# Triangle's sides made with tokens on partitions, half of them kept in SBUF

## The chip, the cores and the metric

The kernel runs on one core of a Trainium2 chip. A core has a matrix engine (TensorE, "PE" in the profile, its weight loads "PEld"), a vector engine (VectorE, "DVE"), an activation engine (ScalarE, "ACT"), GpSimd ("POOL"), a synchronising engine that mostly issues transfers (SyncE, "SP"), and 16 DMA engines that all of them share. The on-chip memories are SBUF and PSUM, each of 128 partitions; TensorE writes PSUM only. The metric is device time in microseconds for one execution. It is given as the median of several runs, and the profile is of one execution more.

## The reference

The input x is one image of 512 by 512 places with 64 channels. Two layers are added to it in turn, each on a group-normalised copy (32 groups, so two channels share a mean and a variance over the whole image).

The first layer is a triangle product. For each place, with LN a normalisation over the 64 channels:

```python
xn = LN(GN(x)) * norm_w + norm_b
m = sequence_mask                                   # 512 numbers, 0 or 1
left  = (xn @ left_w  + left_b)  * m[k] * m[j] * sigmoid(xn @ lgate_w + lgate_b)
right = (xn @ right_w + right_b) * m[k] * m[i] * sigmoid(xn @ rgate_w + rgate_b)
out[i, j, d] = sum over k of left[k, j, d] * right[k, i, d]
out = LN(out) @ out_w + out_b
x = x + out * sigmoid(xn @ ogate_w + ogate_b)
```

(with `onorm` scale and shift in the second LN). The second layer takes a two-dimensional Fourier transform of GN(x), keeps 12 by 12 modes, mixes the channels of each mode with complex weights, transforms back and adds the result.

About half of the mask's 512 entries are one. If at most 256 are, only those rows and columns make `left` and `right`, and the kernel takes its compact path: they are numbered as K = 256 slots. Rows and columns that are masked out get the same constant, the row of `out_b`, in place of a product.

## The kernel before

P is 128, C is 64, K is 256, N is 512. The compact path goes through these stages, each with its order of instructions written out by hand for every engine.

**Index stage** (lines 73 to 137). The mask is counted with a matmul; `n_i` is the number of valid rows and decides between the two paths; `rank_p` numbers the rows, valid ones first; `src_i` and `slot_row` are the resulting lists of rows and slots.

**Gathering stage** (lines 656 to 701). Sixteen tiles `jc` of 32 columns are gathered by GpSimd (`xg` for the two first blocks of ranked rows, `yg` for the two others). TensorE turns every piece into PSUM (L687), VectorE takes its statistics (L688), and ScalarE and GpSimd copy the columns that have a slot into `xc`, a tile of 128 partitions by 257 slots by 2 rows by 64 channels (L673). After tile 8, `make_weights` (L171) folds the norm's scale, shift and mean into the weights. At the end `ab1` holds the group norm's scale and shift of each channel.

**Slots' stage** (lines 704 to 810). `xc` is walked in 64 groups `q` of 4 slots (2 rows a partition: 512 tokens in columns). `channels` turns a group so that channels lie on partitions (rows r = 0, 1 in the two halves of 64) and applies the group norm on ScalarE; `centered` multiplies by a centring matrix, squares, and VectorE sums over channels (L800); every four groups `factors` makes reciprocal roots in nine steps on VectorE, and `spread` sends them by way of HBM (`rs_d`) to all channels (`rbc`). `normed` multiplies (L762), `project` makes gates and sides as 64 x 128 weights against 512 tokens (L768), ScalarE takes the sigmoid with the bias of each partition (L778), VectorE adds the bias to the sides and multiplies (L795), and SP stores `left` and `right` to HBM (L807) with a channel as the outer dimension. The first kind of work on a group runs 13 groups ahead of `project`, the lead-in. The tiles `gates_c`, `sides_c` and `sigc` are single.

**The gap.** After the stage come the bias rows, the two matrices `center_x` and `gate_x`, and the mask in the forms `mask_s` and `mask_own` (lines 813 to 853).

**Triangle** (lines 854 to 915). For every channel `c` both sides are loaded back from HBM four to six channels ahead, turned by eight transposes (L873), copied to SBUF (`left_t` by VectorE L879, `right_t` with the mask by ScalarE L883), and multiplied by four matmuls of 128 x 128 by 256 (L895); VectorE evicts with the masks (L900); SP stores to `tri_d` (L903).

**Products' stage** (lines 990 to 1290, the first 8 of `total_g / 8` rounds). `tri_d` is loaded by channel (`load_product`, L1025), multiplied by a centring matrix and `out_w` (`y_ps`, L1058), normalised, and stored as `u_d`. The units that follow are 32 pieces of the image: each is gathered three units ahead (`load`, called at L1241 to L1245), gets its output gate, is multiplied with `u_d` or the constant row, added to x, stored, and given to the Fourier sums. The tail (from L1316) adds the second layer and writes the output.

TensorE's fp32 matmul appears as two passes (records) in the profile, a transpose as one.

## Time and profile before

| | |
|---|---|
| median of 3 runs | 1782.21 us (1778.42 to 1784.91) |
| profiled execution | 1777.78 us, its span 1776.0 us |
| index and gathering stages | to 200.3 us in the span |
| Slots' stage, lead-in | 200.3 to 227.0 |
| Slots' stage, 64 groups | 227.0 to 440.4 |
| gap before the first triangle product | 440.4 to 453.2 |
| triangle | 453.2 to 619.0 |
| products' stage | 624.6 to 730 |
| units and tail | to 1776.0 |
| busy: TensorE, VectorE, ScalarE, GpSimd | 1567.8, 1413.7, 933.0, 936.5 us |

Reading: a busy share is an average over stages with different limits, so each stage is read by itself, with the waits that end last there. Matmuls are pipelined, so the time of one includes what overlaps with the next; the pitch of a group or a channel says more than the duration of one matmul. A line of groups gives count, total busy time, mean of one in ns, and the idle time before it with what ended it.

### The profile page before, as it was taken

Reading aid. Unit: us, or ns where it says so; the run is one execution under the profiler, and the core shown is the slowest. Engines: PE = TensorE matmul, PEld = TensorE weight load, DVE = VectorE, ACT = ScalarE, POOL = GpSimd, SP = SyncE. Lnnn points to the kernel's source line nnn. Section 1 sums busy time; section 2 is a strip of 40 time slices with the busy share of each in tenths; the row PEclk is TensorE's granted clock in tenths of the full one; section 3 lists DMA queues with packets and bytes.
Section 4 is the critical chain, followed back from the end, with each engine's and each line's share of the span. In section 5 each row is a group of like instructions: output and inputs, shape, how many; then the busy total and the mean of one; then the engine's idle time right before and its main releaser. Section 6 shows DMA issues by size and latency. Waiting matters only on the chain. (4 is left out here: it accounts for less than half of the span.)

```text
span 1776.0 us, 32619 instructions
## 1 busy us (share of the span) xinstructions
PE 1567.8 (88%) x10918; PEld 1242.0 (70%) x10918; DVE 1413.7 (80%) x2982; ACT 933.0 (53%) x1660; POOL 936.5 (53%) x695
## 2 busy tenths in 40 slices
PE   6779799997999978899999999999999977998772
PEld 5667666662899867787888888888888745665341
DVE  7989678887455568688999999999999984865451
ACT  3666566663333266676777777777777742011000
POOL 4666211111000037698999999999999881111110
PEclk9999999999899999899999999999999976555555
DMA  7999278878898789868767767776776699999999
GB/s 281 386 386 388 107 206 227 229 229 245 279 305 303 257 246 347 298 196 296 265 242 257 253 233 259 264 249 239 249 264 244 212 318 400 425 427 427 426 427 385
DMA packets 192593, 518.48 MB, mean 292 GB/s; under 512 B 37664, under 2 KB 104480, under 8 KB 151456
## 3 DMA queue, kind: packets, MB, share of 16 engines
q1 hardware_dynamic: 156112, 295.65, 47.5%
q0 software_dynamic: 32832, 218.45, 33.4%
q10 hardware_dynamic: 3472, 2.20, 0.5%
q8 instruction: 89, 1.46, 0.3%
q14 instruction: 88, 0.72, 0.1%
HBM read 311.60 MB, written 204.60 MB: 291 GB/s over the span
## 5 line engine op out<-in xcount | busy, mean ns | idle before, releaser
L1045 PE MATMUL w_ps<-gate_x,xt_c 128*128 128x128 f32 x2048 | 280.5, 281 | 30.0 <-DVE z_t L1274 28.6
L1113 POOL TENSOR_TENSOR places<-places,z_t 128x1024 f32<-128x1024 f32 x127 | 301.3, 2372 | 8.0
L1045 PEld LDWEIGHTS w_ps<-gate_x,xt_c 128*128 128x128 f32 x2048 | 252.0, 194 | 46.4 <-DVE z_t L1274 44.6
L1045 PE MATMUL c_ps<-center_x,xt_c 128*128 128x128 f32 x2048 | 277.0, 279 | 0.8 <-ACT xt_c L1040 0.4
L1045 PEld LDWEIGHTS c_ps<-center_x,xt_c 128*128 128x128 f32 x2048 | 252.8, 194 | 3.8 <-ACT xt_c L1040 3.0
L1440 PE MATMUL l_ps<-places,rinv 24*128 24x512 f32 x512 | 206.2, 1118 | 29.3 <-DVE places L1447 19.0
L1168 DVE BATCH_NORM_STATS2 stats2c<-places 128x6 f32<-128x128 f32 x1024 | 220.5, 278 | 9.9 <-POOL places L1113 9.9
L1083 DVE TENSOR_REDUCE scratch<-sq_c 128x16 f32<-128x1024 f32 x160 | 194.6, 1216 | 31.1 <-ACT sq_c L1078 16.1
L1221 ACT ACTIVATE z_t<-z_t 128x1024 f32<-128x1024 f32 x128 | 135.5, 1058 | 131.8 <-DVE z_t L1280 131.1
L1440 PEld LDWEIGHTS l_ps<-places,rinv 24*128 24x128 f32 x512 | 119.8, 302 | 110.8 <-DVE places L1447 56.9
L1278 POOL TENSOR_TENSOR z_t<-z_t,bias_row_out 128x1024 f32<-128x1024 f32 x32 | 75.6, 2363 | 226.3 <-PE y_ps L1058 202.1
L1040 ACT ACTIVATE xt_c<-t_ps,ab_xc 128x512 f32<-128x512 f32 x256 | 176.0, 688 | 11.5 <-PE t_ps L1038 10.6
L1274 DVE TENSOR_TENSOR z_t<-w_ps,rs_n 128x512 f32<-128x512 f32 x256 | 172.0, 672 | 6.2 <-PE w_ps L1045 6.1
L1076 ACT ACTIVATE sq_c<-c_ps 128x512 f32<-128x512 f32 x256 | 150.8, 589 | 31.4 <-PE c_ps L1045 30.8
L1280 DVE TENSOR_TENSOR z_t<-z_t,scratch 128x1024 f32<-128x1024 f32 x128 | 156.3, 1221 | 9.9 <-ACT rs_n L1089 3.7
L688 DVE BATCH_NORM_STATS2 stats1c<-x_ps 128x6 f32<-128x512 f32 x256 | 157.1, 682 | 7.7 <-PE x_ps L687 7.4
L1109 POOL TENSOR_TENSOR z_t<-z_t,places 128x1024 f32<-128x1024 f32 x64 | 151.8, 2371 | 14.6 <-ACT z_t L1221 14.4
L1038 PE MATMUL t_ps<-c_ident,places 128*128 128x128 f32 x1024 | 158.4, 278 | 0.0
L1038 PEld LDWEIGHTS t_ps<-c_ident,places 128*128 128x128 f32 x1024 | 118.5, 142 | 51.4 <-issue 51.4
L1447 DVE TENSOR_TENSOR places<-places,l_ps 128x512 f32<-128x512 f32 x176 | 109.3, 682 | 55.2 <-DMA places<-x_h,dst_i 42.1
L1109 POOL TENSOR_TENSOR z_t<-z_t,bias_row_out 128x1024 f32<-128x1024 f32 x63 | 149.4, 2372 | 5.8 <-ACT z_t L1221 5.5
L673 ACT COPY xc<-xg 128x128 f32 x352 | 105.0, 298 | 66.1 <-POOL xc L673 47.1
(214 smaller groups left out, 2557.0 us busy)
## 6 DMA issues: line engine op xcount, KB each, us to landing
x_h<-places SPq DMA_DIRECT2D x64, 1024.0 KB
out_x<-places SPq DMA_DIRECT2D x44, 1024.0 KB
places<-u_d SPq DMA_DIRECT2D x512, 64.0 KB
out_x<-lx_t SPq DMA_DIRECT2D x20, 1024.0 KB
rbc<-rs_d POOLq DMA_DIRECT2D x32, 512.0 KB, 7.1
left_d<-o_c SPq DMA_DIRECT2D x64, 256.0 KB
right_d<-o_c SPq DMA_DIRECT2D x64, 256.0 KB
left_raw<-left_d SPq DMA_DIRECT2D x64, 256.0 KB
```

The lines of the kernel that those rows point to most:

```text
L688: nc.vector.bn_stats(stats[:, 0, 16 * (jc % quarter) + 4 * r + c, :], ps.rearrange("p i k -> p (i k)"))
L1038: nc.tensor.transpose(tps[:, i, :], flat[:, o : o + P], ident)
L1040: nc.scalar.activation(xts[s], tps, AF.Identity, bias=ab1[:, 2:3])
L1045: nc.tensor.matmul(ps[:, 2 * i : 2 * i + 2, :], xts[s][:, i, :], w, start=True, stop=True)
L1076: nc.scalar.activation(sq, cps, AF.Square)
L1083: nc.vector.tensor_reduce(totals[k % 2][:, 8 * (n - 1) : 8 * (n + 1)], sqs.pop(s // 2), AX.X, ALU.add)
L1109: nc.gpsimd.tensor_mul(zs[k, c], zs[k, c], u)
L1113: nc.gpsimd.tensor_add(xr, xr, zs.pop((k, c)))
L1168: nc.vector.bn_stats(st[k // 4][:, g, k % 4, :], x_of(k)[:, :, 2 * g : 2 * g + 2])
L1274: nc.vector.tensor_mul(z[:, 8 * odd : 8 * odd + 8, :], wps, rs)
L1280: nc.vector.tensor_add(z, z, bias_ps["ogate"].unsqueeze(1).to_broadcast([P, 16, C]))
L1440: nc.tensor.matmul(ps.rearrange("p j o -> p (j o)"), rinv[h, b, :], it[h], start=True, stop=True, tile_position=(32 * g, 0),)
```

## The change

The sides are made with tokens on partitions. In `project` the normalised group becomes the weights (64 channels by 128 tokens), and `both_w` (gates and sides beside each other, 64 by 256) is streamed: eight matmuls a group in two halves `h`, each with its PSUM tile `both_c` and sigmoid tile. The bias can no longer be a number of each partition. It becomes a row of `both_w`: the last channel of each half of 64 is made to hold one (times the mask), and what it held is taken out of all channels first, which the centring allows. For that, `shift_of` (GpSimd) makes the last channel times a ratio of the norm's scales, and `shifted` subtracts it (VectorE in the lead-in, GpSimd after); the affine `affine` and the matrix `center_d` leave the last channel out, and the last row of each `spreads` buffer holds the mask, so 63 rows are loaded in place of 64. The factors are multiplied by the mask of their own token, a tenth step.

`leave` writes the sides: channels 0 to 31 of each side back into the group's own place in `xc`, the others to a spill tile that one store sends to `sides_d`. `places`, the buffer of later stages, is now `xc` itself. Triangle reads both operands directly with strides (1 KB between tokens in `xc`, 256 bytes in the loaded quarters, two neighbouring floats for the streamed side), with no transposes, copies or masks. The four spilled quarters are loaded two at the start and one each after channels 32 and 40.

Bias rows, masks and index lists are made in `prepare_slots`, in the gathering stage after tile 8; `center_x` and `gate_x` are made late in the lead-in. The first two units' gathers are issued in triangle. The index stage also counts mask entries other than 0 and 1 and sends those to the general path.

```diff
+        odd = xp.tile([P, 4], F32, name="odd")
+        nc.vector.tensor_tensor(odd, table[:, :, 1], valid, ALU.not_equal)
+        nc.tensor.matmul(cum_ps[:, 8:12], ones, odd, start=True, stop=True)
...
-        nc.vector.tensor_copy(n_i, cum[0:1, 7:8])
+        strange = xp.tile([1, 1], F32, name="strange")
+        nc.vector.tensor_reduce(strange, cum[0:1, 8:12], AX.X, ALU.add)
+        nc.vector.scalar_tensor_tensor(strange, strange, float(N), cum[0:1, 7:8], ALU.mult, ALU.add)
+        nc.vector.tensor_scalar(n_i, strange, float(N), None, ALU.min)
...
+            def prepare_slots(rp):
+                nc.vector.tensor_add(ends_c, ident[:, C - 1 : C], ident[:, P - 1 : P])
+                nc.vector.tensor_scalar(others, ends_c, -1.0, 1.0, ALU.mult, ALU.add)
+                with tc.tile_pool(name="slp", bufs=2, space=PSUM) as rps:
+                    for k, name in enumerate(("gates", "sides")):
+                        sel = rp.tile([P, P], F32, name="sel", tag="scaled")
+                        nc.vector.memset(sel, 0.0)
+                        for r in range(2):
+                            nc.vector.tensor_copy(sel[:, (r + 1) * C - 1 : (r + 1) * C], biases[name])
+                        ps = rps.tile([P, P], F32, name="sel_ps", tag="sel")
+                        nc.tensor.matmul(ps, sel, ident, start=True, stop=True)
+                        for side in range(2):
...
+                            nc.vector.scalar_tensor_tensor(
+                                both_w[...], by(weights[name]), others, by(ps), ALU.mult, ALU.add)
+                    for name in ("ogate", "out"):
...
+                    for r in range(2):
+                        nc.gpsimd.dma_start(u_d[:, K, r, :], rows_of["out"])
...
                     if jc == NJ // 2:
                         make_weights(fc, cp)
+                        prepare_slots(sp)
...
+                spreads = [sp.tile([P, QB, N], F32, name=f"rbc{k}") for k in range(2)]
...
+                def shift_of(q):
+                    tiles_of[q] = wk.tile([P, N], F32, name="shift")
+                    nc.gpsimd.tensor_mul(
+                        by_token(tiles_of[q]), by_token(gts(q))[:, :, C - 1 : C].to_broadcast([P, 8, C]),
+                        ratio.unsqueeze(1).to_broadcast([P, 8, C]),
+                    )
+                def shifted(engine, q):
+                    engine.tensor_sub(gts(q), gts(q), tiles_of.pop(q))
...
-                            rbs[k][h], groups_d[:, r].unsqueeze(0).to_broadcast([C, QB, N])
+                            rbs[k][r * C : (r + 1) * C - 1], groups_d[:, r].unsqueeze(0).to_broadcast([C - 1, QB, N])
...
-                def project(q, k):
-                    ps = pp.tile([P, 2, N], F32, name=k + "_c")
-                    for r in range(2):
-                        h = slice(r * C, (r + 1) * C)
-                        nc.tensor.matmul(ps[:, r, :], weights[k][h], xns[q][h], start=True, stop=True)
+                def project(q, h):
+                    ps = pp.tile([P, 2, 2, 2 * P], F32, name=f"both_c{h}")
+                    for i in range(2):
+                        for r in range(2):
+                            hs = slice(r * C, (r + 1) * C)
+                            o = (2 * h + i) * P
+                            nc.tensor.matmul(ps[:, r, i, :], xns[q][hs, o : o + P], both_w[hs], start=True, stop=True)
+                    sig = sp.tile([P, 2, 2, P], F32, name=f"sigc{h}")
+                    nc.scalar.activation(sig, ps[:, :, :, :P], AF.Sigmoid)
+                    made[q, h] = ps, sig
+                def leave(q, h):
...
+                    nc.vector.tensor_mul(
+                        gts(q)[:, h * 2 * P : (h + 1) * 2 * P].rearrange("p (o k) -> p k o", k=4),
+                        ps[:, :, P : P + C], sig[:, :, :C],
+                    )
...
+                    nc.vector.tensor_mul(
+                        spilt[q].rearrange("p (t h o k) -> p h k t o", t=4, h=2, k=4)[:, h],
+                        by(ps[:, :, P + C :]), by(sig[:, :, C:]),
+                    )
+                    if h == 1:
+                        nc.sync.dma_start(sides_d[:, :, q, :].rearrange("t p f -> p t f"), ...)
...
-                for q in range(-lead - 1, groups):
+                for q in range(-lead - 3, groups + 1):
                     if live(0):
-                        gates = project(q, "gates")
-                        sig = sp.tile([P, 2, N], F32, name="sigc")
-                        nc.scalar.activation(sig, gates, AF.Sigmoid, bias=biases["gates"])
+                        project(q, 0)
                     if live(1):
                         normed(q + 1)
...
+                    if live(-1):
+                        leave(q - 1, 1)
+                    if live(lead + 3):
+                        shift_of(q + lead + 3)
+                    if live(lead + 2):
+                        shifted(nc.vector if q + lead + 2 < lead else nc.gpsimd, q + lead + 2)
...
                     if live(0):
+                        leave(q, 0)
+                        project(q, 1)
...
+                def side(c, s, r):
+                    t, e = divmod(c % 32, 8)
+                    o = 8 * s + e + (16 * t if c < 32 else 0)
+                    v = places if c < 32 else homes[t].rearrange("p q f -> p (q f)")
+                    return v.rearrange("p (j o r b) -> p j o r b", j=P, r=2, b=2)[:, :, o, r, :]
                 def product(c):
...
-                        for kb in range(2):
+                        for r in range(2):
                             nc.tensor.matmul(
-                                ps[:, b, :], lt[:, kb, b * P : (b + 1) * P], rt[:, kb, :], start=(kb == 0), stop=(kb == 1)
+                                ps[:, b, :], side(c, 0, r)[:, :, b], side(c, 1, r), start=(r == 0), stop=(r == 1),
                             )
...
+                load_sides(0)
+                load_sides(1)
+                for c in range(C):
+                    product(c)
+                    if c == 32:
+                        load_sides(2)
+                    if c == 40:
+                        load_sides(3)
+                    if c in (33, 41, 49, 57):
...
+                        nc.vector.memset(places[:, o : o + 1], 0.0)
+                        gather(places[:, o : o + JC * C], tiles, src_i, 2 * units[k][1] + r, units[k][0])
...
-                        if 0 <= v + 3 < len(units):
+                        if EARLY <= v + 3 < len(units):
```

## The prediction

> **What bounds the kernel now.** I read the table of stages first, then the waits inside each stage, then the costliest groups. Five stretches carry the case; the columns are microseconds, busy time and count of each engine, granted clock, DMA share, GB/s.
>
> ```profile
> 125.00:194.60 69.60, 62.14 (x443) 49.14 (x441) 68.68 (x119) 42.04 (x141) 38.21 (x85) 0.96 0.91 354
> 227.00:440.40 213.40, 204.02 (x1134) 114.34 (x1134) 179.47 (x371) 132.43 (x180) 25.44 (x44) 1.00 0.79 230
> 440.40:453.20 12.80, 7.54 (x32) 6.72 (x33) 3.51 (x10) 1.72 (x4) 1.12 (x2) 0.51 0.78 245
> 453.20:619.00 165.80, 164.85 (x1002) 147.91 (x1000) 94.07 (x198) 53.42 (x124) 0.00 (x0) 1.00 0.86 290
> 714.00:730.00 16.00, 10.91 (x73) 9.26 (x72) 6.58 (x9) 5.85 (x12) 9.68 (x6) 0.59 1.01 364
> ```
>
> They are: the end of the gathering stage (third engine column: VectorE busy 68.68 of 69.60); the 64 groups of Slots' stage at 3.33 us; the gap up to the first triangle product; triangle (TensorE busy 164.85 of 165.80, 2.59 us a channel); and the end of the products' stage, where TensorE has holes. Waits of the last four (250 to 400, 456 to 615, 712 to 732): total, times, longest.
>
> ```profile
> ACT sigc L778 <- DVE o_c L795: 35.0, 31, 1.5
> ...
> DVE tri_t L900 <- PE tri_c_ps L895: 72.2, 62, 4.0
> ...
> PE y_ps L1058 <- DMA places<-tri_d: 5.3, 4, 2.6
> ...
> PEld y_ps L1058 <- DMA places<-tri_d: 5.2, 3, 2.8
> ```
>
> In Slots the ring sigmoid (1.11 us), `o_c` (two products), next sigmoid sets the pitch; in triangle VectorE waits for TensorE; at 714 the loads of triangle's result are late, beside gathers of x that GpSimd issued at 708.7, 714.8, 721.0 and 736.6. The durations come from these groups:
>
> ```profile
> L895 PE MATMUL tri_c_ps<-right_t,left_t 128*128 128x256 f32 x512 | 121.4, 380 | 0.0
> L795 DVE SCALAR_TENSOR_TENSOR o_c<-sides_c,b_sides,sigc 128x512 f32<-128x512 f32 x128 | 90.2, 746 | 29.7 <-ACT turned_c L749 11.1 <-ACT sigc L778 6.8 <-ACT xc L723 5.9
> L1274 DVE TENSOR_TENSOR z_t<-w_ps,rs_n 128x512 f32<-128x512 f32 x256 | 172.0, 672 | 6.2 <-PE w_ps L1045 6.1
> L1412 DVE COPY q_sb<-q_ps 128x192 f32<-128x192 f32 x4 | 1.5, 474 | 1.8 <-PE q_ps L1401 1.8
> L1422 DVE COPY places<-it_ps 128x512 f32<-128x512 f32 x2 | 2.0, 1024 | 1.6 <-PE it_ps L1419 1.6
> L1113 POOL TENSOR_TENSOR places<-places,z_t 128x1024 f32<-128x1024 f32 x127 | 301.3, 2372 | 8.0
> ```
>
> **Gathering stage: +11.8.** `prepare_slots` joins VectorE's and TensorE's queues behind `make_weights`. That block now takes 7.1 us (117.5 to 124.7), mostly round trips:
>
> ```profile
> 118.70 0.29 DVE L183 COPY w_sides<-ps_sides 128x128 f32<-128x128 f32 x1 [0.89 <-PE ps_sides L179]
> ```
>
> The new block has a single scratch tile, so it takes two such turns for the selectors (memset and two copies 0.45, turn 0.9, two products 0.45: 1.8 us each), two for the bias rows (copy 0.28, turn 0.85, copy 0.2: 1.35 each), one long one for the mask (2.6), then own/reduce (1.0) and indices (0.8): with 0.2 of preparation, 10.9 us. The next tile's transposes stand behind its matmuls, VectorE's 112 statistics behind its small operations, and from 125 on VectorE has no slack, so all of it stays; 8 to 14. Before, this work lay in the 12.8 us gap under a DMA wait. The two `u_d` rows that move with it stand in GpSimd's queue ahead of the next tile's copies and wait for the bias rows; those copies are due only when the transposes run again, so they cost nothing while the block lasts. Earlier, `odd` and the longer chain to `n_i` add five operations of 0.16 us before the branch: +0.8 (0 to 1.5), no cover, since gathers wait for it.
>
> **Slots' stage.** Before the first group VectorE makes `ratio` (a copy, a matmul turn of 0.9, reciprocal 0.5, product), GpSimd one shift (1.2), VectorE one subtraction (0.7), each with a handover: +4.9 (3 to 6). The following lead-in ran at 1.85 us a group, set by TensorE and ScalarE around `cc_ps`; shifting on GpSimd (1.2) and subtracting on VectorE (0.68 beside 0.69 and the factor steps 0.5) just fit: +1.5 (0 to 4).
> Then 48 groups run with both halves alive. VectorE per group: `normed` 0.68, reduction 0.68, ten factor steps over four groups 0.48, and four products of 256 in place of two of 512. A contiguous one is 0.41 (from the 672 ns row: 0.14 fixed, 1.04 ns an element). These write every fourth float, 16 bytes apart. The rows that write 64 and 128 bytes apart take 1024 ns for 512 and 474 for 192: both 0.14 fixed plus 1.73 ns an element. I take them as nearest: 0.58 each. Sum 4.16; back-to-back operations overlap by some 0.05 (179.47 busy against 206 of summed rows), leaving 3.75; a little for GpSimd's hiccups makes 3.8. GpSimd itself has two operations of 512 (half of 2372: 1.2 each) and its share of DMA issues (1.76 per four groups) and of the wait until the factors land (2.0): 3.35, just covered. TensorE streams as many columns as before; only its weight loads double, and `y_ps`, with the same 64-row loads, ran 30 to 32 passes in 2.05 to 2.39 us (two row halves at once): under 3.3. SP issues one store a group in place of two, and four small mask rows ahead of them while it is idle. ScalarE 2.6. The last 16 groups need 0.68 + 4 x 0.58 less overlap: 2.85.
> 48 x 3.8 + 16.5 x 2.85 = 229.4 against 213.4: **+16**. Floor: contiguous price, GpSimd binds at 3.45, then 2.4: 205, -8. Ceiling: GpSimd and VectorE's two-SBUF products exclude each other, 4.3 and 3.1: 257, +44.
>
> Two rules speak here. The Trainium skill (Advanced Engine Details and Errata, SBUF Cachelines) says that a 16-byte line wants two hits: 16 bytes apart is then a full miss, and so is every column of triangle's new weights. If a weight column also took 1.73 ns, a load of 128 would take 0.22 us against 0.214 of streaming and the sum would move by +3. The same skill (DMA: Bandwidth & Descriptors, Why a DMA increments its semaphore by 16 and not by 1) says that a transfer takes the largest number of engines up to 16 that divides its rows: 63 rows of `rbc` would use 9, its 7.1 us landing (the row) could become 12.6, and the first `normed` would be 3 us later. The sum below uses neither.
>
> **Gap: -12.3.** Stores' landing, loads, transposes and evictions between 440.4 and 453.2 go; the first product needs only the last `leave`.
>
> **Triangle: -41.** Transposes (8 passes of 128), one VectorE copy and two ScalarE copies a channel go; 8 passes of 256 columns remain. 16 passes with 3072 columns took 2.59 us, so a column takes 0.84 ns and a channel 1.72; I take 1.75 for the strided reads: 112. VectorE (0.9) lies beside. But SP now queues two loads of 4.2 MB ahead of the first result store, in the same queue. No row shows such a block in triangle; the nearest is the tail, where a 1 MB store, 2.5 us of traffic at 427 GB/s, lands 39 us after its issue behind others:
>
> ```profile
> 1651.20 39.13 DMA out_x<-lx_t
> ```
>
> 8.4 MB at 390 to 427 GB/s with 4 us until Slots' stores land and 2 to land itself puts the first store at about 27 us. Three output tiles and six PSUM tiles let TensorE run nine channels, 15.8 us: it stalls 11 to 12 us, once; the later two loads, 10 us each, are nearly covered (+1). 112 + 12.8 = 125 against 165.8. Floor: no block, 1.72: -55. Ceiling 0: weights that don't hide (below). DMA has 38 MB: at 290 GB/s for a share of 0.86, 112 us, not the bound.
>
> **Products' stage: -7.** Four gathers (4 MB) are done in triangle, issued by GpSimd, idle there, behind four one-column memsets on VectorE. The waits of 714 to 730 (10.5 on two queues, overlapping) shrink; 0 to -11.
>
> **Sum.** 0.8 + 10.9 + 4.9 + 1.5 + 16 - 12.3 - 41 - 7 = -26. The profiled execution took 1777.8 us (span 1776.0 and 1.8 around it), 4.4 below the median of the runs, 1782.2. Against itself 1752; against the median 1756, which I forecast.
>
> **Rivals.**
> 1. *Strided writes and queued loads are nearly free.* For it: the eight-byte steps of `right_t` on ScalarE cost little (487 ns for 256). Against: both VectorE rows above. Slots -8, triangle -54: sum -63, 1719; one of both, 1732 or 1743. Chance 0.20 for below 1735.
> 2. *Slower: triangle's weights, single floats 256 to 1024 bytes apart, load too slowly to hide under the 0.214 us of streaming.* For it: no matmul here reads its weights so. Against: even at 1.73 ns a column they tie. Without triangle the sum is +15, and a slower channel covers more of the block, so it decides from 2.24 us a channel, 0.28 a pass. With a load of 0.1 us wholly behind each stream, 2.5: triangle 165, total 1797. Chance 0.17.
> 3. *GpSimd and VectorE exclude each other in Slots.* Slots +44, sum +2: 1784, no change. For it: no stage here runs both with two SBUF inputs each. Chance 0.10.
> Also possible, 0.04: `prepare_slots` hides under DMA after all, 1745, inside the forecast's range.
>
> **How the numbers follow.** The forecast has 0.53 (own range 1735 to 1777). The range of 1722 to 1796 holds it, the upper half of rival 1, rival 3 and most of rival 2. 0.3% (5.3 us) is about what a measurement here tells from no change: faster is under 1777 (forecast nearly whole, rival 1: 0.72), same to 1787 (rival 3's middle and edges: 0.09), slower beyond (rival 2 and rival 3's end: 0.19).
>
> **What would show it.** The strided products near 580 ns (410 in rival 1), Slots' pitch 3.8 with VectorE hardly idle; a stretch of 11 us on VectorE between the statistics near 125; triangle's passes at 0.214 us with one hole of about 12 us after nine channels (rival 2: no hole, a longer pitch); no TensorE wait for `tri_d` near the first gathered unit. Wrong, above all, if passes exceed 0.28 us or Slots' pitch exceeds 4.3.

## The result, and the profile after

The change made the kernel slower: 1860.69 us in the median of four runs (1854.0 to 1861.59) against 1781.76 us for the kernel before on the same chip (1778.42 to 1784.91). The ratio is 1.0435, 95% interval 1.0404 to 1.0466. The forecast was a faster kernel, 1756 us, with a range of 1722 to 1796 us; the change went the other way, past the end of that range. The profiled execution took 1860.4 us, its span 1858.6 us.

The two spans differ by 82.6 us. Cut at the first product of Slots' projection, at the first product of triangle and at the first `y_ps` of the products' stage, they compare so with the prediction's terms:

| stretch | before | after | difference | forecast |
|---|---|---|---|---|
| up to `ab1` (index, gathering) | 200.3 | 212.6 | +12.3 | +11.7 |
| set-up and lead-in of Slots | 26.7 | 37.6 | +10.9 | +6.4 |
| Slots' 64 groups and the gap | 226.2 | 311.5 | +85.3 | +3.7 |
| triangle, to the first `y_ps` | 171.4 | 149.6 | -21.8 | -41 |
| the rest | 1151.4 | 1147.3 | -4.1 | -7 |

So 82 us of the 109 that are missing lie in one stage, and 19 in triangle. These are the stretches of the kernel after, in the order of the columns shown before: `prepare_slots`, the gathering behind it, Slots from the first projection to the first triangle product, triangle, and the end of the products' stage.

```profile
126.40:137.60 11.20, 7.22 (x27) 6.05 (x28) 5.63 (x31) 2.56 (x9) 3.14 (x8) 0.50 0.81 318
138.00:207.00 69.00, 63.81 (x432) 45.02 (x430) 68.83 (x121) 39.34 (x132) 38.16 (x85) 0.99 0.79 306
250.20:561.70 311.50, 232.37 (x1646) 185.22 (x1647) 286.92 (x511) 149.12 (x245) 150.29 (x143) 0.90 0.35 105
561.70:704.70 143.00, 118.24 (x512) 114.29 (x512) 54.14 (x131) 0.00 (x0) 3.91 (x4) 0.92 0.71 263
797.00:812.00 15.00, 11.95 (x143) 10.21 (x144) 12.61 (x15) 10.48 (x21) 11.96 (x6) 1.00 0.87 299
```

In Slots VectorE is busy for 286.92 of 311.50 us (it was 179.47 of 213.40), TensorE for only 232. The waits of the kernel after between 262 and 500 us name VectorE behind TensorE's, and GpSimd behind its weight loads:

```profile
ACT sigc L878 <- PE both_c L876: 81.0, 72, 6.2
...
PE both_c L876 <- DVE o_c L891: 41.4, 27, 4.6
...
PEld xc_ps L824 <- POOL xc L819: 23.1, 16, 3.4
```

About 45.5 groups go through in these 238 us, 5.2 us each; the forecast had 3.8, and named a pitch above 4.3 as a sign that it was wrong. The groups of VectorE and then of GpSimd in the same window tell why:

```profile
L891 DVE TENSOR_TENSOR o_c<-both_c,sigc 128x256 f32<-128x256 f32 x93 | 59.4, 639 | 0.0
L886 DVE TENSOR_TENSOR xc<-both_c,sigc 128x256 f32<-128x256 f32 x93 | 58.7, 631 | 0.7 <-ACT sigc L878 0.7
L865 DVE TENSOR_TENSOR xnc<-xc,rbc 128x512 f32<-128x512 f32 x46 | 50.0, 1086 | 4.2 <-PE both_c L876 4.2
L928 DVE TENSOR_REDUCE total<-sqc 128x8 f32<-128x512 f32 x46 | 31.2, 678 | 7.9 <-ACT sqc L836 7.8
L215 DVE SCALAR_TENSOR_TENSOR rq_h<-rq_h 128x32 f32<-128x32 f32 x11 | 15.1, 1375 | 0.0
L216 DVE SCALAR_TENSOR_TENSOR rq_y<-rq_h,rq_y 128x32 f32<-128x32 f32 x11 | 14.7, 1332 | 0.4
L219 DVE SCALAR_TENSOR_TENSOR rq_w<-rq_w,rq_y 128x32 f32<-128x32 f32 x11 | 8.5, 776 | 0.4
L218 DVE TENSOR_TENSOR rq_w<-rq_y,rq_v 128x32 f32<-128x32 f32 x11 | 6.9, 629 | 0.4
...
L819 POOL TENSOR_TENSOR xc<-xc,shift 128x512 f32<-128x512 f32 x45 | 58.2, 1293 | 0.0
L813 POOL TENSOR_TENSOR shift<-xc,ratio 128x512 f32<-128x512 f32 x44 | 51.2, 1164 | 2.6
```

The strided products are near the forecast (631 and 639 ns against 580), and the reduction has kept its time. But `xnc` takes 1086 ns, and factor steps of 32 elements take up to 1375 ns. Before, they took this long, in a window of Slots:

```profile
L762 DVE TENSOR_TENSOR xnc<-xc,rbc 128x512 f32<-128x512 f32 x47 | 32.0, 681 | 0.0
...
L209 DVE SCALAR_TENSOR_TENSOR rq_h<-rq_h 128x32 f32<-128x32 f32 x11 | 2.1, 191 | 0.4
```

A stretch of the timeline of the kernel after (start, duration) shows what a step of 32 elements does in a microsecond:

```profile
339.20 1.40 POOL L813 TENSOR_TENSOR shift<-xc,ratio 128x512 f32<-128x512 f32 x1
339.61 1.04 DVE L215 SCALAR_TENSOR_TENSOR rq_h<-rq_h 128x32 f32<-128x32 f32 x1
340.56 1.26 POOL L819 TENSOR_TENSOR xc<-xc,shift 128x512 f32<-128x512 f32 x1
340.68 1.19 DVE L216 SCALAR_TENSOR_TENSOR rq_y<-rq_h,rq_y 128x32 f32<-128x32 f32 x1
341.90 1.11 POOL L813 TENSOR_TENSOR shift<-xc,ratio 128x512 f32<-128x512 f32 x1
```

The first step begins during GpSimd's product and ends at 340.65, 50 ns after that product's end at 340.60; the second ends at 341.87, after GpSimd's next operation ends at 341.82. It looks as if a VectorE operation with two inputs in SBUF waits until GpSimd's whole operation is over, however short it is itself. That was rival 3, with a price of 44 us. The runs had to show whether it is the cause and the whole cause.

### The profile page after: what moved, and what is told of

Same layout as the page of the kernel before. It is cut to its first block, busy times and chain, and to the rows that moved or that the text cites. A ratio compares the mean times of both kernels' runs of the same rounds, so it can differ in the third digit from the quotient of the medians.

```text
span 1858.6 us, 32419 instructions
## 1 busy us (share of the span) xinstructions
PE 1547.5 (83%) x10928; PEld 1274.3 (69%) x10928; DVE 1500.4 (81%) x3105; ACT 894.7 (48%) x1596; POOL 1079.2 (58%) x810
## 5 line engine op out<-in xcount | busy, mean ns | idle before, releaser
L1181 POOL TENSOR_TENSOR xc<-xc,z_t 128x1024 f32<-128x1024 f32 x127 | 301.2, 2372 | 8.0
L1508 PE MATMUL l_ps<-xc,rinv 24*128 24x512 f32 x512 | 206.3, 1118 | 29.6 <-DVE xc L1515 18.9
L1236 DVE BATCH_NORM_STATS2 stats2c<-xc 128x6 f32<-128x128 f32 x1024 | 220.7, 279 | 8.3 <-POOL xc L1181 8.3
L1508 PEld LDWEIGHTS l_ps<-xc,rinv 24*128 24x128 f32 x512 | 119.6, 301 | 111.3 <-DVE xc L1515 57.4
L876 PE MATMUL both_c<-both_w,xnc 64*128 64x256 f32 x1024 | 146.3, 425 | 55.8 <-DVE o_c L891 54.6
L1108 ACT ACTIVATE xt_c<-t_ps,ab_xc 128x512 f32<-128x512 f32 x256 | 176.1, 688 | 13.3 <-PE t_ps L1106 12.3
L876 PEld LDWEIGHTS both_c<-both_w,xnc 64*128 64x128 f32 x1024 | 105.4, 203 | 81.8 <-issue 46.1
L1177 POOL TENSOR_TENSOR z_t<-z_t,xc 128x1024 f32<-128x1024 f32 x64 | 151.8, 2371 | 15.0 <-ACT z_t L1289 14.9
L1106 PE MATMUL t_ps<-c_ident,xc 128*128 128x128 f32 x1024 | 158.0, 277 | 0.0
L1106 PEld LDWEIGHTS t_ps<-c_ident,xc 128*128 128x128 f32 x1024 | 118.5, 142 | 51.7 <-issue 51.5
L1515 DVE TENSOR_TENSOR xc<-xc,l_ps 128x512 f32<-128x512 f32 x176 | 109.5, 683 | 54.6 <-DMA xc<-x_h,dst_i 44.0
```

The costliest lines, as they stand in the source:

```text
L876: nc.tensor.matmul(ps[:, r, i, :], xns[q][hs, o : o + P], both_w[hs], start=True, stop=True)
L1106: nc.tensor.transpose(tps[:, i, :], flat[:, o : o + P], ident)
L1108: nc.scalar.activation(xts[s], tps, AF.Identity, bias=ab1[:, 2:3])
L1177: nc.gpsimd.tensor_mul(zs[k, c], zs[k, c], u)
L1181: nc.gpsimd.tensor_add(xr, xr, zs.pop((k, c)))
L1236: nc.vector.bn_stats(st[k // 4][:, g, k % 4, :], x_of(k)[:, :, 2 * g : 2 * g + 2])
```

## Experiments on Slots' stage

Theory S: GpSimd's two shift operations and VectorE's operations with two SBUF inputs keep each other out. Rivals: GpSimd's results come too late for TensorE; or VectorE's strided writes cost more than their durations tell.

**Without the shift.**

```diff
 def shift_of(q):
-    tiles_of[q] = wk.tile([P, N], F32, name="shift")
-    nc.gpsimd.tensor_mul(...)
+    return
 def shifted(engine, q):
-    engine.tensor_sub(gts(q), gts(q), tiles_of.pop(q))
+    return
```

> The changed kernel without GpSimd's shift and without the subtraction (left out: the last channel is not taken out of the others, so the sides have wrong values; nothing else is left out). Exclusion theory (VectorE's instructions with two SBUF inputs stand still while GpSimd runs one): normed back to 0.68 us, the factor steps to 0.19, the 48 groups from 5.3 to 4.1 us, lead-in about 10 us shorter: 1785 to 1795 us. Rival (GpSimd is merely late with its own results, and TensorE and ScalarE wait for them): the same time, 1785 to 1795, so this run gives the price of the shift, not its cause. Third view (strided writes and four products are the cost, not the shift): 1850.

Measured: 1769.84 us, ratio 0.9946 (0.9928 to 0.9963) to the kernel before; that is 15 us under the range that both theories gave, and far from the third view's 1850. Groups of VectorE between 262 and 450 us:

```profile
L887 DVE TENSOR_TENSOR o_c<-both_c,sigc 128x256 f32<-128x256 f32 x104 | 66.4, 639 | 0.0
...
L861 DVE TENSOR_TENSOR xnc<-xc,rbc 128x512 f32<-128x512 f32 x52 | 35.6, 684 | 1.9 <-PE both_c L872 1.9
...
L215 DVE SCALAR_TENSOR_TENSOR rq_h<-rq_h 128x32 f32<-128x32 f32 x12 | 2.3, 189 | 0.0
```

`xnc` and the steps are back at their old durations, the strided products are not changed, 52 groups go through in 188 us (3.6 us each). From the first projection to triangle it takes 232.1 us, 2 more than the prediction had for all of it. The shift costs 91 us; the prediction had its set-up and lead-in at 6.4 us and let the rest run beside VectorE for almost nothing. As was said before the run, this gives the price of the shift, not its cause.

**One-input operations on GpSimd.** Two copies of 512 elements stand in place of the product and the subtraction.

```diff
-    nc.gpsimd.tensor_mul(by_token(tiles_of[q]), ..., ...)
+    nc.gpsimd.tensor_copy(tiles_of[q], gts(q))
...
-    engine.tensor_sub(gts(q), gts(q), tiles_of.pop(q))
+    engine.tensor_copy(gts(q), tiles_of.pop(q))
```

> The changed kernel with GpSimd's product and subtraction replaced by two copies of the same 512 elements at the same places and with the same dependences (left out: the shift, so the sides have wrong values). Exclusion theory, if it takes two SBUF inputs on GpSimd's side: normed 0.68, steps 0.19, total 1790 to 1805, although GpSimd still delivers as late as its copies take. If exclusion comes from any GpSimd instruction: little gain, 1840 or more. Rival (GpSimd merely late): the total goes with the length of GpSimd's copies; if a copy takes as long as 1.1 us, 1850, with VectorE's instructions short only where GpSimd is idle.

Measured: 1799.99 us, ratio 1.0124 (1.0084 to 1.0165). Two groups between 262 and 450 us:

```profile
L813 POOL COPY shift<-xc 128x512 f32<-128x512 f32 x44 | 30.6, 696 | 2.0
...
L218 DVE TENSOR_TENSOR rq_w<-rq_y,rq_v 128x32 f32<-128x32 f32 x11 | 6.9, 629 | 0.4
```

The copies take 696 and 625 ns; `xnc` is at 702 ns, but the four long steps still take 531 to 629 ns. So a GpSimd operation that reads SBUF once also holds VectorE up, for its own, shorter time. The total lies in the range that was expected if only two inputs on GpSimd's side mattered, but the steps are not back at 0.19 us: that condition is not met.

**The factor steps' operands in PSUM.** Two of the steps' tiles and the mask lie in a PSUM tile, with one copy more, so that no step has two inputs in SBUF. GpSimd keeps its work; `xnc` keeps its two inputs.

```diff
-    rss[k], steps = rsqrt_steps(rp, totals.pop(k), 1.0 / C, EPS, [P, QB * 8])
+    y = scr[:, P + 32 * (k % 2) : P + 32 * (k % 2) + 32]       # scr: a tile in PSUM
+    h = scr[:, 2 * P + 32 * (k % 2) : 2 * P + 32 * (k % 2) + 32]
+    own = scr[:, 3 * P : 3 * P + 2]...
+    todo.extend([..., lambda: vec.tensor_mul(h, w, y), lambda: vec.tensor_copy(w, h), ...])
```

> The changed kernel with the factor chain rearranged so that no instruction of it has two SBUF inputs (two of its tiles and the mask lie in PSUM, one copy more per four groups); GpSimd's work is as before. Exclusion theory: the steps fall from up to 1.36 us to about 0.2 to 0.25 each, normed stays near 1.0; the sum of the excess on the steps is 52 us, so the total falls to 1805 to 1820. Rival (GpSimd merely late, the long steps only fill a wait): 1850 to 1861.

Measured: 1810.52 us, ratio 1.018 (1.0142 to 1.0217). Groups between 262 and 450 us:

```profile
L821 POOL TENSOR_TENSOR xc<-xc,shift 128x512 f32<-128x512 f32 x44 | 60.6, 1377 | 0.0
...
L883 DVE TENSOR_TENSOR xnc<-xc,rbc 128x512 f32<-128x512 f32 x44 | 48.5, 1101 | 0.0
...
L859 DVE SCALAR_TENSOR_TENSOR rc_ps<-rq_w,rc_ps 128x32 f32<-128x32 f32 x11 | 2.1, 195 | 0.4
```

The steps are at 174 to 195 ns although GpSimd does exactly as much as before; `xnc` still takes 1101 ns. 50 of the 91 us are gone by where the operands lie, with no instruction taken from GpSimd and one added to VectorE. That settles against GpSimd being merely late. It is late as well: in the same 188 us TensorE's weight loads for `xc_ps` wait 20.4 us for GpSimd's subtraction. How the 41 us that remain divide between this and `xnc` is not measured.

**The kernel before, with GpSimd made busy.** Two products of 512 elements an iteration, of a tile that nothing else uses.

```diff
 # in the kernel before, in the loop over q
+    if live(lead + 1):
+        for _ in range(2):
+            nc.gpsimd.tensor_mul(extra, fixed, fixed)
 ...
     channels(q + lead + 1)
```

> The kernel before, complete, with two products of 512 elements a lead iteration added on GpSimd, of tiles that nothing else uses. Theory (GpSimd's and VectorE's operations with two inputs in SBUF keep each other out, whatever the layout of the change): `xnc` goes from 0.68 to about 1.0 us, the factor steps from 0.19 us to 0.4 or more; GpSimd's 2.4 us and VectorE's 0.68 + 3 * 0.19 us can't overlap any more, so that the group takes 0.6 to 1.5 us more over 64 groups: 1818 to 1875 us. Rival (the lengthening belongs to the layout or to the waits of the change): durations on VectorE stay within 10%, 1775 to 1790 us.

Measured: 1827.82 us, ratio 1.0247 (1.0212 to 1.0282). Groups between 262 and 420 us:

```profile
L801 DVE SCALAR_TENSOR_TENSOR o_c<-sides_c,b_sides,sigc 128x512 f32<-128x512 f32 x76 | 53.4, 744 | 7.3 <-PE sides_c L768 5.1 <-ACT sigc L781 2.0 <-ACT xc L723 0.2
L762 DVE TENSOR_TENSOR xnc<-xc,rbc 128x512 f32<-128x512 f32 x39 | 33.9, 868 | 0.0
...
L212 DVE TENSOR_TENSOR rq_w<-rq_y,rq_v 128x32 f32<-128x32 f32 x10 | 10.3, 1025 | 0.0
...
L789 POOL TENSOR_TENSOR extra<-fixed 128x512 f32<-128x512 f32 x76 | 86.6, 1140 | 5.4
```

Work that nobody waits for costs the kernel before 44 us. `xnc` (two SBUF inputs) and the steps stretch, `o_c` (PSUM and SBUF) stays at 744 ns, where it was 746. GpSimd also issues the transfers of the factors, but `xnc` never waited for them in this window (idle before it 0.0). The change's layout is not needed for it.

**The shift on VectorE.**

```diff
-    nc.gpsimd.tensor_mul(by_token(tiles_of[q]), ...)
+    nc.vector.tensor_mul(by_token(tiles_of[q]), ...)
...
-    shifted(nc.vector if q + lead + 2 < lead else nc.gpsimd, q + lead + 2)
+    shifted(nc.vector, q + lead + 2)
```

> The change, complete, with both operations of the shift on VectorE in every group, none on GpSimd. Theory (GpSimd's 2.4 us a group hold VectorE up longer than the same work takes on VectorE itself): `xnc` back to 0.68 us, the factor steps to 0.19 us; two operations of some 0.6 us more a group on VectorE, which was busy 48.2 of 50 us without the shift: 3.6 + 1.15 = 4.75 us a group instead of 5.3, so 64 * 1.15 = 74 us above the run without shift, 1840 to 1856 us. Rival (the work itself is too much wherever it is, or the two operations take over 0.9 us each on VectorE): 1865 us or more.

Measured: 1828.19 us, ratio 1.026 (1.0236 to 1.0285), 33 us less than the change. VectorE between 262 and 450 us:

```profile
L819 DVE TENSOR_TENSOR xc<-xc,shift 128x512 f32<-128x512 f32 x41 | 28.1, 686 | 0.0
L813 DVE TENSOR_TENSOR shift<-xc,ratio 128x512 f32<-128x512 f32 x40 | 27.6, 690 | 0.0
L865 DVE TENSOR_TENSOR xnc<-xc,rbc 128x512 f32<-128x512 f32 x40 | 27.6, 689 | 0.0
```

The pitch is 4.65 us (40.5 groups in 188 us), near the 4.75 expected; the total came out under the expected range, 1840 to 1856: that charged 1.15 us to all 64 groups, where only the 48 of the main loop carry a shift (48 times 1.15 is 55; measured are 58 above the run without shift). The same work takes 0.69 us twice on VectorE and 1.16 and 1.29 us on GpSimd: moving it to the busiest engine is better than leaving it on the idle one.

**Writes in order.**

```diff
-    .rearrange("p (o k) -> p k o", k=4)
+    .rearrange("p (k o) -> p k o", k=4)
...
-    spilt[q].rearrange("p (t h o k) -> p h k t o", t=4, h=2, k=4)[:, h]
+    spilt[q].rearrange("p (h k t o) -> p h k t o", t=4, h=2, k=4)[:, h]
```

> The change, but the four products of `leave` write their 256 elements in the order in which they read them, without 16-byte steps; the values then lie at other places than triangle takes them from, so the sides are mixed up (same work, other values). Theory (VectorE sets Slots' pitch, and the strided write is a price of its own, beside GpSimd's shift): each product falls from 0.63 to about 0.42 us, as the two products of 512 before had 0.81 us for 512; four of them a group over 64 groups give 0.21 * 4 * 64 = 54 us less, at least 40: 1805 to 1822 us, with `xnc` still at 1.0 us. Rival (GpSimd sets the pitch, VectorE only follows it): under 10 us less, 1850 to 1862 us.

Measured: 1848.72 us, ratio 1.0368 (1.0319 to 1.0416). The products fell to 417 and 414 ns, as expected, but the total by 12 us only, between the two forecasts and close to the rival's. Pitch 4.9 us. While GpSimd runs, time saved on VectorE is partly spent waiting: its idle time before the reduction rose to 15.4 us in the window, and more steps meet GpSimd (the last one, `rq_out`, went from 431 to 897 ns).

## Experiments on triangle

TensorE in triangle, in the kernel after: start, length of a run of passes, count, and in brackets the hole before it.

```profile
561.73 15.89 PE L964 MATMUL tri_c_ps<-xc 128*128 128x256 f32 x72 [1.92 <-DVE o_c L891]
589.47 42.65 PE L964 MATMUL tri_c_ps<-xc 128*128 128x256 f32 x184 [11.85 <-DVE tri_t L969]
...
652.72 12.39 PE L964 MATMUL tri_c_ps<-sides 128*128 128x256 f32 x48 [3.34 <-DVE tri_t L969]
...
675.86 12.77 PE L964 MATMUL tri_c_ps<-xc 128*128 128x256 f32 x48 [7.29 <-DVE tri_t L969]
```

72 passes are nine channels, 15.89 us, then a hole of 11.85: the forecast, 11 to 12 us after nine channels. But 3.34 and 7.29 us follow at the later loads, where it had 1. The wait is for the stores of the results (waits of 561 to 705 us):

```profile
DVE tri_t L969 <- DMA tri_d<-tri_t: 61.0, 13, 20.4
```

The prediction put this down to SP's queue: the stores stand behind the loads. The rival: the DMA engines are full while a load runs, whoever issued it.

**Loads from another queue.**

```diff
-    nc.sync.dma_start(homes[t], sides_d[t])
+    nc.scalar.dma_start(homes[t], sides_d[t])
```

> The changed kernel with the four loads of spilled sides issued on ScalarE's queue in place of SP's. Queue theory (result stores stand behind the loads in one queue): VectorE's waits for stores of 20, 12 and 15 us shrink to a few us, TensorE's holes of 11.9, 3.3 and 7.3 us go, triangle from 143 us to 118 to 124, total 1838 to 1845. Rival (stores are late because the loads take the DMA engines, whatever the queue): holes of similar size, total 1855 to 1861.

Measured: 1861.62 us, ratio 1.0463 (1.0425 to 1.05). VectorE's wait for stores is 67.3 us in 17 waits, the longest 12.3 instead of 20.4, and TensorE's holes (0.84, 9.15, 2.15, 8.93 us) add up to 21.1 us, against 22.5.

```profile
DVE tri_t L969 <- DMA tri_d<-tri_t: 67.3, 17, 12.3
```

That is the rival's forecast: the one queue is not the cause. The table of stages of the change itself shows the engines full (share 1.02), then the stores alone (0.39):

```profile
570.00:580.00 10.00, 7.62 (x36) 7.32 (x34) 0.00 (x0) 0.00 (x0) 0.00 (x0) 1.00 1.02 442
...
590.00:600.00 10.00, 10.00 (x36) 8.93 (x35) 6.72 (x17) 0.00 (x0) 0.00 (x0) 0.76 0.64 236
600.00:610.00 10.00, 10.00 (x48) 10.00 (x48) 4.90 (x12) 0.00 (x0) 0.00 (x0) 1.00 0.39 141
```

**Loads in eight pieces, one every second channel.**

```diff
-    nc.sync.dma_start(homes[t], sides_d[t])
+    qs = slice(8 * k, 8 * k + 8)
+    nc.sync.dma_start(homes[t][:, qs], sides_d[t][:, qs])
...
+    if c < 32 and c % 2 == 0:
+        load_sides(c // 16, c // 2 % 8)
+    if 32 <= c < 48 and c % 2 == 0:
+        load_sides(2, (c - 32) // 2)
+    if 40 <= c < 56 and c % 2 == 1:
+        load_sides(3, (c - 41) // 2)
```

> The change, with each load of 4 MB in triangle cut into eight of 0.5 MB that are issued two channels apart between the result stores. Theory (the DMA engines are what the stores wait for: share 1.0 while a load runs, 0.4 between): both streams together stay under what the engines move, the holes of 11.9, 3.3 and 7.3 us on TensorE go, triangle takes 1.73 us a channel throughout: 16 to 24 us less, 1836 to 1846 us. Rival (volume decides, the holes only move): TensorE idles at other places by the same sum, 1853 to 1863 us.

Measured: 1857.37 us, ratio 1.0414 (1.0377 to 1.0451). The first hole is gone, but the total is the rival's: two new holes follow, the first behind channels 40 to 47, in which two loads ran at a time:

```profile
564.10 55.61 PE L965 MATMUL tri_c_ps<-xc 128*128 128x256 f32 x256 [1.92 <-DVE o_c L891]
...
660.95 15.89 PE L965 MATMUL tri_c_ps<-xc 128*128 128x256 f32 x64 [13.61 <-DMA tri_d<-tri_t]
684.90 15.86 PE L965 MATMUL tri_c_ps<-sides 128*128 128x256 f32 x64 [8.07 <-DMA sides<-sides_d]
```

**The late pieces spaced evenly.**

```diff
+    late_pieces = {32 + 7 * k // 5: k for k in range(16)}
...
+    if c in late_pieces:
+        load_sides(2 + late_pieces[c] // 8, late_pieces[c] % 8)
```

> The change, with the loads in eight pieces each as in the run before; the pieces of the third and fourth load go out evenly, 1.4 channels apart from channel 32 to 53, instead of doubled up between channels 40 and 48. Theory (the DMA engines are the limit only where loads and stores together ask for over about 400 GB/s: with the doubled pieces 0.75 MB in 1.73 us, 433 GB/s, there was a hole of 13.6 us; at 300 GB/s, channels 0 to 31, none): 0.61 MB in 1.73 us ask for 351 GB/s, no hole over 3 us, triangle's products end 125 to 130 us after their start instead of 143: 1840 to 1848 us. Rival (pieces are never free, the stall of a load only moves): holes of 10 us or more in all after channel 40, 1852 to 1860 us.

Measured: 1843.56 us, ratio 1.0348 (1.0323 to 1.0373), 17 us less than the change.

```profile
558.57 57.27 PE L965 MATMUL tri_c_ps<-xc 128*128 128x256 f32 x256 [1.92 <-DVE o_c L891]
...
646.88 15.85 PE L965 MATMUL tri_c_ps<-xc 128*128 128x256 f32 x64 [3.42 <-DMA xc<-sides_d]
672.58 16.82 PE L965 MATMUL tri_c_ps<-sides 128*128 128x256 f32 x64 [9.85 <-DMA tri_d<-tri_t]
```

From the first product to the first `y_ps` it now takes 138.0 us instead of 149.6; so about 12 of the 17 us are triangle's, the rest lies before and behind it. The time is as the theory had it, the condition is not: holes of 13 us remain where loads and stores ask for an estimated 351 GB/s (0.61 MB in 1.73 us). This estimate overlooked the first units' gathers. GpSimd issues four in triangle, 4.19 MB together, and three of them, at 622.9, 640.6 and 656.6 us, fall among the late pieces. From 625 to 665 us the engines' share is 0.96 to 1.01 while they move 353 to 383 GB/s; from 565 to 615, with pieces and stores only, it was 0.81 to 0.95 at 266 to 309 GB/s, and there was no hole. So the stall comes with full engines and not with the order of one queue; what it would be without the gathers, no run shows.

## Experiments for a better kernel

**Bias by small products, no shift.** All 64 channels stay; each accumulation is opened by a bf16 product of two rows, the mask as weights against the bias in two parts. The first form of the pieces of loads is in it too.

```diff
+    for r in range(2):
+        rows = slice(r * C, r * C + 2)
+        nc.tensor.matmul(ps[:, r], mask_b[rows, r * P : (r + 1) * P],
+                         both_b[rows].unsqueeze(1).to_broadcast([2, 2, 2 * P]), start=True, stop=False, ...)
     ...
-    nc.tensor.matmul(ps[:, r, i, :], xns[q][hs, o : o + P], both_w[hs], start=True, stop=True)
+    nc.tensor.matmul(ps[:, r, i, :], xns[q][hs, o : o + P], both_w[hs], start=False, stop=True, ...)
```

> A complete kernel without any shift: channel 63 stays, the factors spread to all 64 rows as before, and the bias comes by a bf16 product of two rows (mask as weights; bias in two bf16 parts) that opens each accumulation, four of 512 columns a group; the loads in pieces as well. Theory: Slots loses GpSimd's 91 us (the run without shift: 1769.8), the loads' 18 and the set-up's 5; the four products are new on TensorE, which was busy 47.2 of 50 us without the shift, so nearly all of their time is on the path: if two of them run at a time as the 64-row products do, 2 * 0.2 to 2 * 0.39 us a group, 26 to 50 us over 64 groups: 1773 to 1797 us. Rival (they run one after another, 4 * 0.39 us): 1845 us or more.

Measured: 1800.42 us, ratio 1.0098 (1.0065 to 1.0131), 3 us above the expected range. A product of 512 columns takes 384 ns, two at a time; TensorE is the bound, busy for all 188 us of its window:

```profile
262.00:450.00 188.00, 188.00 (x1421) 129.70 (x1419) 168.89 (x375) 111.34 (x187) 19.27 (x33) 1.00 0.49 125
```

**The same with spaced pieces, and masks and bias rows made in the lead-in.**

```diff
+    later = [mask_rows, mask_columns, lambda: bias_row("ogate"), lambda: bias_row("out"), places_of]
...
+    if q > -lead and later:
+        later.pop(0)()
```

> The complete kernel without shift (bias by bf16 products, 1800.4 us), with two edits: the late pieces spaced evenly as in the run with spaced pieces, and the parts of `prepare_slots` that are not needed for the weights (mask row and columns, the two bias rows, the places) moved from the gathering, where VectorE sets the pace, into Slots' lead-in, where it waits. Theory: the holes of triangle after channel 32 go (12 to 20 us), and about 7 of the 11 us of `prepare_slots`: 1773 to 1784 us, level with the kernel before or slightly under it. Rival (VectorE's operations in the lead-in push the first groups back by as much; holes stay): 1792 us or more.

Measured: 1793.94 us, ratio 1.0063 (1.0044 to 1.0083). `ab1` was ready 7.2 us earlier (its last copy began at 210.0 instead of 217.2), but the first projection came only 0.9 us earlier (244.4 instead of 245.3): the lead-in takes the time back, as the rival had it. Triangle kept holes of 2.8 and 11.6 us.

**Shift on VectorE, writes in order, spaced pieces.** The sides are written in the order in which they are read, and triangle's reads follow.

```diff
-    return v.rearrange("p (j o r b) -> p j o r b", j=P, r=2, b=2)[:, :, o, r, :]
+    return v.rearrange("p (j r b o) -> p j o r b", j=P, r=2, b=2)[:, :, o, r, :]
```

> A complete kernel with three edits on the change: both operations of the shift on VectorE (1828.2 us alone), triangle's loads in evenly spaced pieces (17 us less), and the sides written in the order in which the products read them, with triangle's reads changed to match, so that its streamed side takes single floats 64 or 256 bytes apart in place of two neighbours. Theory (with GpSimd silent VectorE alone sets Slots' pitch, 49.3 of 50 us busy; then the strided writes' price is all on the path, which it was not beside GpSimd: there 0.86 us a group were worth only 12 us): products 0.415 us in place of 0.63, pitch from 4.35 to about 3.55 us, where TensorE's 3.3 is next; 64 * 0.8 = 51 us: 1828 - 51 - 17 = 1760 us, 1750 to 1778, under the kernel before; triangle stays at 1.73 us a channel. Rival 1 (the streamed side pays for its single floats, 0.1 us or more a pass, eight passes a channel): 1800 us or more. Rival 2 (VectorE stays the bound for another reason, products at 0.6 us): 1805 to 1815 us.

Measured: 1873.83 us, ratio 1.0531 (1.0517 to 1.0545). Slots did shrink: 252.5 us from first projection to triangle, against 280.7 with the shift on VectorE alone. That is the strided writes' price once GpSimd is silent, 28 us, about half of the 55 that 0.215 us a product would make; why only half is not shown. Triangle took it back three times over, as rival 1 had it:

```profile
L965 PE MATMUL tri_c_ps<-xc 128*128 128x256 f32 x255 | 109.8, 607 | 0.0
L965 PEld LDWEIGHTS tri_c_ps<-xc 128*128 128x128 f32 x253 | 74.2, 293 | 34.6
```

A pass whose streamed side takes single floats, 64 or 256 bytes between the two that were neighbours, runs at a pitch of 0.43 us (256 passes in 110.40 us), with no hole; with two neighbouring floats it was 0.217 (256 in 55.61 us, in the run with pieces). No version tried beats the kernel before with the whole computation.

## Why the prediction was wrong

**The step that failed: "a little for GpSimd's hiccups makes 3.8".** VectorE's own operations came out nearly right: without the shift a group takes 3.6 us, and Slots with the gap 232.1 us, where the prediction had 229.9. There is some luck in it, since two errors cancel: the strided products took 0.63 to 0.64 us instead of 0.58, and operations overlapped more than was allowed for (the rows of that window add up to 223 us in 180 of busy time). What was missing, put at 0.05 us for "hiccups", is that GpSimd's 2.45 us a group shut out VectorE's operations with two SBUF inputs. Per group, from the two windows, `xnc` rose by 0.40 us (1086 less 684 ns) and the ten steps over four groups by 0.92 us, and VectorE's idle time grew from 0.16 to 0.34 us; that is 1.5 of the 1.6 us by which 3.6 became 5.2. The shift costs 91 us with GpSimd and 58 with VectorE doing all of it (1828 against 1770).

**Rival 3 had the mechanism and the wrong price.** Its 4.3 us a group comes without a working and names VectorE's products only, not the steps of 32 elements, 0.19 us by themselves, each of which can also wait for the whole of a GpSimd operation of over 1.1 us. For its chance the prediction had only that no stage before runs both kinds at once, which is no evidence either way. The Trainium skill (SBUF — State Buffer, Who interferes with whom) states the rule: a VectorE instruction with two SBUF inputs contends with a GpSimd instruction that reads SBUF, and whichever comes second waits for the whole of the other. This case agrees: 1025 ns for a step of 32 beside GpSimd's 1140, and 195 ns with an operand in PSUM. The prediction priced the case without this rule, which speaks directly against the change.

**Set-up and lead-in: +10.9 instead of +6.4.** The same cause shows there in part: the last operation on `affine` and the one on `center_d` ran beside the first shifts and took 1.07 and 1.16 us, where they took 0.16 and 0.28 in the run without shift; the third subtraction took 1.53 us where most took 0.68. `center_d` has one wide input and one number a partition, so a second wide input does not seem to be needed. Without the shift the first projection came 7.8 us earlier.

**Gathering: right.** `prepare_slots` took 11.1 us (10.9), and VectorE was busy for 68.83 of the 69 us behind it, so nothing hid it.

**Triangle: the stall was foreseen, its cause was wrong and three sizes were off.** The first hole was right to 0.1 us, by a sum (8.4 MB of loads ahead of the first store) that comes out alike whether a queue or the engines hold the store back. The cause given, one queue, was wrong: with the loads on another queue the holes add up to nearly the same, and full DMA engines go with them. The holes at the later loads were 10.6 us instead of 1, TensorE lost another 7 us after its holes (118.7 us of passes where 64 channels at 1.75 make 112), and the wait before the first `y_ps` was 8.9 us where it had been 6.6. Together they make nearly all of the 19 us.

**Rival 2: false, as weighed.** The weights did load more slowly, 294 ns in place of 191, yet a pass kept its 0.217 us, so they still hide. The rule of the Trainium skill (Advanced Engine Details and Errata, SBUF Cachelines), that a line of 16 bytes wants two hits, is seen in the run with all three edits, on the streamed side, where it does count: one float of each line, and 0.43 us a pass.

**Products' stage: right,** 98.4 us to the end of its `y_ps` in place of 104.3, -6 against -7. **63 rows:** the rule on engines that divide the rows (the Trainium skill, DMA: Bandwidth & Descriptors, Why a DMA increments its semaphore by 16 and not by 1) made no difference here: `rbc` landed in 6.5 us in place of 7.1. The same section makes an exception for some copies that GpSimd issues, which the prediction did not mention; GpSimd issues `rbc`, but no run shows whether it falls under it.

## What to carry to other kernels

Before work is given to an idle GpSimd, list VectorE's instructions in the same stretch that read SBUF twice, the smallest first: each may last as long as GpSimd's whole operation, so the count matters and not the size. If the work must stay, move one operand of those instructions to PSUM, or do the work on VectorE: 50 and 33 us here. And the layout that is cheap for the writer has to be priced at the reader in the same sum: 28 us saved in Slots cost 90 in triangle (220.5 us of passes and holes against 130.8 with the same pieces).

## What the hardware showed beyond expectation

- A GpSimd copy of 0.6 to 0.7 us holds VectorE's steps up as a product does (0.19 to 0.6 us); one input in SBUF on GpSimd's side is enough.
- Behind a hole TensorE runs slower for a while: after the one of 11.85 us the clock was granted at 0.76, and 36 passes went through in 10 us instead of 48. This stall cost more than its length.
- The clock granted to TensorE in Slots was 0.90 where it was 1.00 before; there TensorE is busy for 232 of 311 us in place of 204 of 213.
